# Bilinear sampling of a deformable convolution: hat weights on input rows replaced by ramps on differences of neighbouring rows

## The chip, the cores and the metric

The program runs on one core of a Trainium2 chip: TensorE (PE, matmul), VectorE (DVE), ScalarE (ACT), GpSimd (POOL), and SyncE (SP), which here only issues transfers. Times are device microseconds (us) of one launch. The time before is the median of three launches; the profile is of one further execution, whose span is its own.

## The reference

Four layers are applied to x of 16 images, 32 channels, 128 x 128, each as a residual on a group-normalised input. The change lies in layer 1, a deformable convolution with nine taps. Cut to what matters:

```python
y = weight * yk + y_new                 # row positions, one per image, tap, row and column
ys = jnp.clip(y_map, 0.0, Hi - 1.0)     # x positions are whole numbers: a column each
...
for dy in (0.0, 1.0):                   # the two rows next to y
    yi = y0 + dy
    w = 1.0 - jnp.abs(gy - yi)
    out = out + feat[:, yi, xc] * w
...
out = conv2d(deformed, dsc_w, dsc_b, stride=(K, 1))
return group_norm(out, gn_w, gn_b, gn_w.shape[0] // 4)
```

A sample at row position y of a column is a linear interpolation between two rows x[r]. It can be written in two ways over all 128 rows: as a sum of x[r] times the hat max(0, 1 - |y - r|), or as x[0] plus the sum of (x[r+1] - x[r]) times the ramp min(1, max(0, y - r)).

## The kernel before

The stages of the program run one after the other: layer 0, the offsets of layer 1, the scan of layer 1, the sampling of layer 1 (`layer1_sample`), layer 2, layer 3. The sampling goes image by image, 16 images of 32 blocks; a block is four output columns, that is 512 sample positions for each of the nine taps. The gather is a matmul: the stationary side is an input column `xt[:, :, xc]` (128 rows x 32 channels), the moving side the weights of all 128 rows for the 128 positions of a column.

For each block m the weights come from three places. For taps 0 to 3 (`near`, tile `ya`) PE spreads one row of the position map `Y` over 128 partitions with a one-hot matrix `sel` (L1121), ACT subtracts the row number and takes the absolute value on the way out of PSUM (L1122), and DVE makes the hat, min(d, 1) - 1 (`hats`, L1126). For taps 4 to 7 (tile `yd`) a transfer of 1 MB brings the positions already repeated over the partitions (`fetch`, L1111), ACT takes the absolute value (`absolutes`, L1242) and DVE makes the hat. Tap 8 (`eighth`, tile `h8`) is as `ya`, once for four blocks. The minus sign of the hat is in the convolution's weights `w4`, `w8`.

Then PE gathers (`taps`, L1133, 16 matmuls for taps 0 to 3 and 16 for taps 4 to 7), and DVE copies each result from PSUM to `ds` (L1280, L1286). For every four blocks there follow the last tap (L1307), the convolution over the taps (`convolve`, L1168, L1173, L1176), and transposes into the image's output `ob` (`turn`, L1185, L1186). While the next image runs, `finish` normalises `ob` piece by piece, one step after each block, adds the residual `xt` (L1233) and sends `ob` out by a transfer that POOL issues (L1234).

Order: the instructions of PE, DVE and ACT in the loop keep the program's order (`in_order`). SP's transfers are placed by the framework's scheduler; SP itself works through them in a fixed order, and a transfer that waits holds up those behind it. `yd` has four buffers, and the loads run three blocks ahead; `xt`, 2 MB per image in four quarters of 8 channels (L1099, rows of 512 bytes), has two buffers, as have `Y` and `Y8` (L1091, L1095). PSUM: two buffers `pb` for the spreads, two `pd` for gathers.

Two other lines are used below as measures: L797 in the scan loads a tile `dd` of 128 partitions from 8 rows of `dm`, each repeated 16 times, and L666 loads `xa` and `xb` in pieces of 72 and of 24 rows.

Of the kernel before, what the change touches and what calls it, by code (L numbers as in the profile page):

```python
# [10 lines left out]
F32 = mybir.dt.float32  # L11
AF = mybir.ActivationFunctionType
ALU = mybir.AluOpType
# [1017 lines left out]
def layer1_sample(tc, w, x1, x2, ymap, sb1, batches=range(B)):  # L1031
# [6 lines left out]


    nc = tc.nc  # L1040
    V, S, M = nc.vector, nc.scalar, nc.tensor.matmul
    W4 = 4 * HW
    NB = HW // 4
    batches = list(batches)
    with ExitStack() as ctx:
# [9 lines left out]
        nrow = load(nc, cp, w["nrow"], "nrow")  # L1055
        avg = cp.tile([P, P], F32, name="avg", tag="avg")
        V.memset(avg, 1.0 / P)

        sel = cp.tile([P, 32, P], F32, name="sel", tag="sel")

        cb = cp.tile([P, NG, 4, 2], F32, name="cb", tag="cb")
        with tc.tile_pool(name="ct", bufs=1) as tp:
            e32 = load(nc, tp, w["eye32"], "eye32")
            V.tensor_copy(sel, e32.unsqueeze(2).to_broadcast([P, 32, P]))
# [22 lines left out]
        def open_image(b):  # L1087
            im = images[b] = {}
            g, j = divmod(b, 4)
            im["Y"] = Y = yp.tile([P, W4], F32, name="Y", tag="Y")  # L1090
            nc.sync.dma_start(Y, ym(b)[0:4].rearrange("k (n f) -> (k n) f", f=W4))  # L1091
            im["Y8"] = Y8 = yp.tile([P, W4], F32, name="Y8", tag="Y8")
            y8 = ym(b)[8].rearrange("(s q f) -> q s f", q=4, f=W4)
            for q in range(4):
                nc.sync.dma_start(Y8[32 * q : 32 * q + 8], y8[q])  # L1095
            im["xt"] = xt = xp.tile([P, T, HW], F32, name="xt", tag="xt")
            xg = x1[g][T * j : T * j + T].rearrange("o (r c) -> r o c", c=HW)
            for q in range(4):
                nc.sync.dma_start(xt[:, 8 * q : 8 * q + 8], xg[:, 8 * q : 8 * q + 8])  # L1099

            s = cb[:, g, j, 0:1]
            im["w4"] = w4 = sp.tile([P, 2, T], F32, name="w4", tag="w4")
            V.tensor_scalar(w4, dw4[:, :, 0:T], s, -1.0, ALU.mult, ALU.mult)
            im["w8"] = w8 = sp.tile([P, P], F32, name="w8", tag="w8")
            V.tensor_scalar(w8, dw8, s, -1.0, ALU.mult, ALU.mult)

        def fetch(m):
            b, n = order[m]
# [3 lines left out]
                yd, ym(b)[4:8, n * W4 : n * W4 + W4].unsqueeze(0).to_broadcast([P, 4, W4])  # L1112
            )

        def spread(dst, Y, n, k):

            for h in range(2):
                pb = psb.tile([P, 2, W4], F32, name="pb", tag="pb")
                for a in range(2):
                    q = 32 * (2 * h + a)  # L1120
                    M(pb[:, a], sel[q : q + k, n], Y[q : q + k], start=True, stop=True)  # L1121
                S.activation(dst[:, 2 * h : 2 * h + 2], pb, AF.Abs, bias=nrow)  # L1122

        def hats(t):

            V.tensor_scalar(t, t, 1.0, 1.0, ALU.min, ALU.subtract)  # L1126

        def sample(pd, b, todo):

# [61 lines left out]
        def finish(b):  # L1191

            g, j = divmod(b, 4)
            im = images[b]
            ob, xt = im["ob"], im["xt"]
# [44 lines left out]
        def absolutes(m):  # L1240
            yd = blocks[m]["yd"]
            S.activation(yd, yd, AF.Abs, bias=nrow)  # L1242

        def near(m):
            b, n = order[m]
            blocks[m]["ya"] = ya = hp.tile([P, 4, W4], F32, name="ya", tag="ya")
            spread(ya, images[b]["Y"], n, 32)

        def eighth(b, s):
            h8 = hp.tile([P, 4, W4], F32, name="h8", tag="h8", bufs=2)  # L1250
            spread(h8, images[b]["Y8"], s, 8)
            images[b]["h8", s] = h8

        open_image(batches[0])
        NM = len(order)
        for m in range(min(3, NM)):
            fetch(m)
        with in_order(tc, nc.tensor, nc.vector, nc.scalar):
            eighth(batches[0], 0)
            near(0)  # L1260
            absolutes(0)
            near(1)
            hats(images[batches[0]]["h8", 0])
            hats(blocks[0]["ya"])
            hats(blocks[0]["yd"])
            done = iter(())
            for m in range(NM + 6):
                b, n = order[m] if m < NM else (None, m - NM)
                if m < NM:
                    bl = blocks[m]  # L1270
                    bl["ds"] = dp.tile([P, 2, W4], F32, name="ds", tag="ds", bufs=6)
                    if n == 12 and m + NB < NM:
                        open_image(order[m + NB][0])
                    if m + 3 < NM:
                        fetch(m + 3)
                    pd = taps(m, 0, bl["ya"])
                    if m + 1 < NM:
                        absolutes(m + 1)
                        hats(blocks[m + 1]["ya"])
                    V.tensor_copy(bl["ds"][:, 0], pd.rearrange("p i r -> p (i r)"))  # L1280
# [5 lines left out]
                    V.tensor_copy(bl["ds"][:, 1], pd.rearrange("p i r -> p (i r)"))  # L1286
                s, i = divmod(n, 4)
                if i == 0 and 4 <= m <= NM:
                    bb, nn = order[m - 4]
# [14 lines left out]
                elif i == 3 and m < NM:  # L1304
# [3 lines left out]
                    images[b]["ds8"] = ds8  # L1308
                    if m + 1 < NM:
                        nb_, nn = order[m + 1]  # L1310
                        hats(images[nb_]["h8", nn // 4])
                next(done, None)
            for _ in done:
                pass
# [982 lines left out]
def pack(inp):  # L2297
# [105 lines left out]
    w["nrow"] = -np.arange(P, dtype=f)[:, None]  # L2403

    def conv(a):
        return _diag(a.reshape(a.shape[0], a.shape[1], 9).transpose(1, 2, 0), 4)
# [97 lines left out]
```

## Time and profile before

| | us |
|---|---|
| three launches: median (lowest, highest) | 16867.01 (16856.64, 16888.87) |
| profiled execution, span | 16843.7 |
| layer 0, about 0 to 5600 | 5600 |
| offsets of layer 1, 5600 to 6050 | 450 |
| scan of layer 1, 6050 to 10,850 | 4800 |
| sampling of layer 1, 10,850 to 14,024 | 3174 |
| layer 2, 14,024 to 14,600 | 576 |
| layer 3, 14,600 to the end | 2243 |

The boundaries are read from the first and last instructions of the stages' lines and rounded. A row of instructions in the profile reads: line, engine, operation, output tile <- input tiles, output shape <- input shape, count; busy time in us and the mean of one in ns; idle time of the engine just before them, and who ended it. The stage is 512 blocks long. By the starts of L1242, one per block, an image takes 189 to 198 us, and four blocks some 23.4 us where nothing is late.

### The profile page before, as it was taken

What the parts mean: (1) busy time and instruction counts of PE and PEld (TensorE: products, weight loads), DVE (VectorE), ACT (ScalarE), POOL (GpSimd) and SP (SyncE); (2) the same over time, 40 slices, a digit from 0 to 9 for tenths busy, and PEclk for the clock granted to TensorE, in tenths of its full rate; (3) what the DMA queues carried; (4) which work ended last, traced back from release to release, by engine and by line L of the source; (5) the groups of instructions that cost most, each with busy time, mean ns of one, the idle gap of its engine ahead of it and who ended that gap; (6) DMA issues with size and microseconds to landing.
All of it is one profiled execution on the core that took longest, in us unless ns stands there. A gap on an engine that the chain in (4) does not pass through costs nothing. (4 is left out here: it accounts for less than half of the span.)

```text
span 16843.7 us, 301825 instructions
## 1 busy us (share of the span) xinstructions
PE 14662.1 (87%) x113386; PEld 5677.8 (34%) x113386; DVE 14631.9 (87%) x14520; ACT 12582.5 (75%) x25308; POOL 9561.6 (57%) x17517
## 2 busy tenths in 40 slices
PE   8999999989999888988888888899999997688966
PEld 3333333333333222222222222255555553234421
DVE  9999999999999669999999999888888887788622
ACT  8999999999999557777777677688898883466411
POOL 8999999999999238778887788500000000000012
PEclk9999999999999989899999999899999898788977
DMA  0000000000000854445454445578877789644456
GB/s 22 13 12 13 13 17 13 13 12 13 18 13 8 136 139 164 154 161 163 168 166 163 156 161 168 159 187 197 200 199 194 193 192 195 129 79 83 79 147 201
DMA packets 1553471, 1898.99 MB, mean 113 GB/s; under 512 B 158053, under 2 KB 879710, under 8 KB 1543239
## 3 DMA queue, kind: packets, MB, share of 16 engines
q1 hardware_dynamic: 1440582, 1701.94, 38.7%
q0 software_dynamic: 31552, 127.40, 2.1%
q10 hardware_dynamic: 79872, 50.36, 1.2%
q8 instruction: 892, 14.61, 0.4%
q14 instruction: 573, 4.69, 0.1%
HBM read 1560.92 MB, written 229.64 MB: 106 GB/s over the span
## 5 line engine op out<-in xcount | busy, mean ns | idle before, releaser
L235 POOL TENSOR_SCALAR Rp<-su,nv 128x128 f32<-128x128 f32 x15360 | 5406.1, 371 | 167.7 <-PE pS L241 132.9
L239 ACT ACTIVATE Ra<-su,bv 128x128 f32<-128x128 f32 x15360 | 4625.8, 389 | 405.9 <-PE pS L241 402.6
L224 DVE TENSOR_TENSOR Rd<-pu,nv 128x2048 f32<-128x2048 f32 x2176 | 4856.6, 2275 | 19.6 <-PE pS L241 18.6
L241 PE MATMUL pS<-Rd,zw 128*32 128x512 f32 x17408 | 2794.8, 606 | 380.1 <-DVE Rd L224 379.4
L828 DVE TENSOR_TENSOR_SCAN hh<-dd,state,pd 128x512 f32<-128x512 f32 x2304 | 2823.3, 1267 | 152.6 <-PE py L862 9.6
L849 POOL TENSOR_TENSOR hh<-hh,bc 128x2048 f32<-128x2048 f32 x512 | 2319.0, 4530 | 451.2 <-DVE state L836 437.9
L1234 POOL DMA_DIRECT2D x<-ob x64 | 92.4, 1443 | 3106.4 <-DVE ob L1233 2769.9
L813 PE MATMUL pd<-du,spread 32*128 32x512 f32 x4608 | 1348.8, 659 | 553.3 <-DVE hh L828 545.7
L805 ACT ACTIVATE dd<-dd,m_a 128x512 f32<-128x512 f32 x2304 | 1513.1, 713 | 328.5 <-DMA dd<-dm 322.4
L823 DVE TENSOR_TENSOR pd<-pd,bc 128x1024 f32<-128x1024 f32 x1152 | 1401.0, 1216 | 53.4 <-ACT bc L786 51.4
L241 PE MATMUL pS<-Rp,zw 128*32 128x512 f32 x7680 | 1310.7, 597 | 25.3 <-POOL Rp L235 25.2
L1242 ACT ACTIVATE yd<-yd,nrow 128x2048 f32<-128x2048 f32 x512 | 1239.7, 2421 | 47.6 <-DMA yd<-ymap 47.5
L1122 ACT ACTIVATE ya<-pb,nrow 128x1024 f32<-128x1024 f32 x1024 | 1188.4, 1251 | 86.5 <-PE pb L1121 85.4
L241 PE MATMUL pS<-Ra,zw 128*32 128x512 f32 x7680 | 1235.7, 600 | 0.0
L1121 PE MATMUL pb<-Y,sel 32*128 32x512 f32 (+1 forms) x5120 | 1083.6, 742 | 167.5 <-ACT ya L1122 164.2
L241 PEld LDWEIGHTS pS<-Rd,zw 128*32 128x32 f32 x17408 | 580.8, 109 | 1487.5 <-DVE Rd L224 928.7
L813 PEld LDWEIGHTS pd<-du,spread 32*128 32x128 f32 x4608 | 372.8, 190 | 1594.7 <-DVE hh L828 714.4
L1126 DVE TENSOR_SCALAR yd<-yd 128x2048 f32<-128x2048 f32 x512 | 724.2, 1414 | 191.8 <-ACT yd L1242 190.9
L1126 DVE TENSOR_SCALAR ya<-ya 128x2048 f32<-128x2048 f32 x512 | 756.7, 1478 | 9.2 <-ACT ya L1122 7.6
L1133 PE MATMUL pd<-ya,xt 128*32 128x128 f32 x16384 | 690.7, 311 | 42.7 <-DVE ds L1286 31.3
L1133 PEld LDWEIGHTS pd<-yd,xt 128*32 128x32 f32 x16384 | 539.2, 178 | 469.9 <-issue 231.5
L1839 PE MATMUL ps<-t,W 128*128 128x512 f32 x1280 | 627.8, 637 | 64.2 <-DVE W L1819 56.5
(426 smaller groups left out, 23147.3 us busy)
## 6 DMA issues: line engine op xcount, KB each, us to landing
dd<-dm SPq DMA_DIRECT2D x2304, 256.0 KB
yd<-ymap SPq DMA_DIRECT2D x512, 1024.0 KB
hw<-x SPq DMA_DIRECT2D x192, 512.0 KB
dm<-dt POOLq DMA_DIRECT2D x192, 256.0 KB, 3.6
w<-d SPq DMA_DIRECT2D x512, 73.1 KB
xb<-tok SPq DMA_DIRECT2D x248, 144.0 KB
x<-in_x SPq DMA_DIRECT2D x64, 512.0 KB
x<-o SPq DMA_DIRECT2D x128, 256.0 KB
```

Source lines behind the costliest of these rows:

```text
L224: nc.vector.tensor_tensor(R, st["pu"].unsqueeze(1).to_broadcast([P, 4, 4, HW]), nv[:, :, i::32].rearrange("p t q -> p q t").unsqueeze(3).t ...
L235: nc.gpsimd.tensor_scalar(R[:, q, k], su[:, k], 3.4028234e38, nv[:, k, c], ALU.min, ALU.max)
L239: nc.scalar.activation(R[:, q, k], su[:, k], AF.Relu, bias=bv[:, k, c])
L241: nc.tensor.matmul(st["pS"][32 * q : 32 * q + 32], zw[:, 31 - i : 63 - i], R[:, q], start=first, stop=False, tile_position=(0, 32 * q), sk ...
L805: S.activation(dd[:, r], dd[:, r], AF.Exp, scale=acol[:, dr, d : d + 1])
L813: nc.tensor.matmul(pd[:, a], spread[e, k], st["du"][n][e], start=True, stop=True)
L823: V.tensor_mul(pd, pd, bm.unsqueeze(1).to_broadcast([P, 2, CH]))
L828: V.tensor_tensor_scan(hh[:, r, s], dd[:, r, s], pd[:, a, s], st["state"][:, 4 * i + r : 4 * i + r + 1], ALU.mult, ALU.add,)
L849: G.tensor_mul(hh, hh, st["bc"][1, n].unsqueeze(1).to_broadcast([P, 4, CH]))
L1126: V.tensor_scalar(t, t, 1.0, 1.0, ALU.min, ALU.subtract)
L1133: M(pd[32 * q : 32 * q + 32, i], xt[:, :, xc], h, start=True, stop=True, tile_position=(0, 32 * q),)
L1242: S.activation(yd, yd, AF.Abs, bias=nrow)
```

## The change

- `hats` on rows becomes ramps on differences. The weights are now min(1, max(0, y - r)) for r = 0 to 126, and row 127 carries a constant weight of one for row 0 of the image. `xt` therefore holds rows 1 to 127 in partitions 0 to 126 and row 0 in partition 127 (two transfers per quarter, 127 rows and one row); POOL then subtracts the unshifted rows, which come in a tile `xq` of their own with two buffers (`quarter`, `differ`). The next image's subtractions are written in blocks 24 to 27 of the image before it; POOL's instructions keep the program's order too.
- The residual in `finish` reads a fresh load of `xq`, since `xt` no longer holds the input.
- The row number is subtracted by the spread product: `Y` is split in `Y0` and `Y1`, with 16 rows and a row of ones in each group of 32 partitions, and `sel` has the step (0, -1, -2, ..., and 1 for row 127) in the row that meets the ones. The spread has 17 rows in place of 32 (or of 8 for tap 8). `Y8` has its 8 rows twice.
- `ya` is made by one DVE operation from PSUM (two for a block, 128 x 1024 each) in place of an ACT and a DVE pass.
- For `yd` and `h8` ACT takes Relu in place of Abs and DVE takes the minimum with one.
- The two copies of gathers to `ds` move from DVE to ACT, and `ramps` stands behind the next spread in the program.

```diff
-            im["Y"] = Y = yp.tile([P, W4], F32, name="Y", tag="Y")
-            nc.sync.dma_start(Y, ym(b)[0:4].rearrange("k (n f) -> (k n) f", f=W4))
...
+            for h, key in enumerate(("Y0", "Y1", "Y8")):
+                im[key] = Y = yp.tile([P, W4], F32, name=key, tag=key)
+                for q in range(4):
+                    p = 32 * q
+                    if h < 2:
+                        nc.sync.dma_start(Y[p : p + 16], yk[q, h])
+                    else:
+                        nc.sync.dma_start(Y[p : p + 8], y8[q])
+                        nc.sync.dma_start(Y[p + 8 : p + 16], y8[q])
+                nc.sync.dma_start(Y[16:P:32], w["one_rows"])
...
-                nc.sync.dma_start(xt[:, 8 * q : 8 * q + 8], xg[:, 8 * q : 8 * q + 8])
+                o = slice(8 * q, 8 * q + 8)
+                nc.sync.dma_start(xt[0 : P - 1, o], xg[1:P, o])
+                nc.sync.dma_start(xt[P - 1 : P, o], xg[0:1, o])
...
+        def quarter(b, q):
+            g, j = divmod(b, 4)
+            xq = xp.tile([P, 8, HW], F32, name="xq", tag="xq")
+            xg = x1[g][T * j + 8 * q : T * j + 8 * q + 8].rearrange("o (r c) -> r o c", c=HW)
+            nc.sync.dma_start(xq, xg)
+            return xq
+
+        def differ(b, q):
+            xt = images[b]["xt"][0 : P - 1, 8 * q : 8 * q + 8]
+            G.tensor_sub(xt, xt, quarter(b, q)[0 : P - 1])
...
-                    M(pb[:, a], sel[q : q + k, n], Y[q : q + k], start=True, stop=True)
-                S.activation(dst[:, 2 * h : 2 * h + 2], pb, AF.Abs, bias=nrow)
-
-        def hats(t):
-
-            V.tensor_scalar(t, t, 1.0, 1.0, ALU.min, ALU.subtract)
+                    M(pb[:, a], sel[q : q + 17, n], Y[q : q + 17], start=True, stop=True)
+                if whole:
+                    V.tensor_scalar(dst[:, 2 * h : 2 * h + 2], pb, 0.0, 1.0, ALU.max, ALU.min)
+                else:
+                    S.activation(dst[:, 2 * h : 2 * h + 2], pb, AF.Relu)
+
+        def clamps(t):
+
+            V.tensor_scalar_min(t, t, 1.0)
...
+                xq = quarter(b, q)
...
-                V.tensor_add(ob[:, o], ob[:, o], xt[:, o])
+                V.tensor_add(ob[:, o], ob[:, o], xq)
...
-            S.activation(yd, yd, AF.Abs, bias=nrow)
+            S.activation(yd, yd, AF.Relu, bias=step)
...
-        with in_order(tc, nc.tensor, nc.vector, nc.scalar):
+        with in_order(tc, nc.tensor, nc.vector, nc.scalar, nc.gpsimd):
...
+                    if 24 <= n < 28 and m + NB < NM:
+                        differ(order[m + NB][0], n - 24)
...
-                    if m + 1 < NM:
-                        absolutes(m + 1)
-                        hats(blocks[m + 1]["ya"])
-                    V.tensor_copy(bl["ds"][:, 0], pd.rearrange("p i r -> p (i r)"))
+                    S.copy(bl["ds"][:, 0], pd.rearrange("p i r -> p (i r)"))
                     if m + 2 < NM:
                         near(m + 2)
+                    if m + 1 < NM:
+                        ramps(m + 1)
                     pd = taps(m, 4, bl["yd"])
                     if m + 1 < NM:
-                        hats(blocks[m + 1]["yd"])
-                    V.tensor_copy(bl["ds"][:, 1], pd.rearrange("p i r -> p (i r)"))
+                        clamps(blocks[m + 1]["yd"])
+                    S.copy(bl["ds"][:, 1], pd.rearrange("p i r -> p (i r)"))
```

More of the change, by code (lines that the diff above doesn't have):

```diff
@@ L1040, in layer1_sample @@
     nc = tc.nc
-    V, S, M = nc.vector, nc.scalar, nc.tensor.matmul
+    V, G, S, M = nc.vector, nc.gpsimd, nc.scalar, nc.tensor.matmul
     W4 = 4 * HW
@@ L1054, in layer1_sample @@
         ident = load(nc, cp, w["ident"], "ident")
-        nrow = load(nc, cp, w["nrow"], "nrow")
+        step = load(nc, cp, w["step"], "step")
         avg = cp.tile([P, P], F32, name="avg", tag="avg")
         V.memset(avg, 1.0 / P)
-        sel = cp.tile([P, 32, P], F32, name="sel", tag="sel")
+        sel = cp.tile([P, 16, P], F32, name="sel", tag="sel")
         cb = cp.tile([P, NG, 4, 2], F32, name="cb", tag="cb")
         with tc.tile_pool(name="ct", bufs=1) as tp:
-            e32 = load(nc, tp, w["eye32"], "eye32")
-            V.tensor_copy(sel, e32.unsqueeze(2).to_broadcast([P, 32, P]))
+            pick = load(nc, tp, w["pick"], "pick")
+            srow = load(nc, tp, w["step_row"], "step_row")
+            V.tensor_add(
+                sel, pick.unsqueeze(2).to_broadcast([P, 16, P]),
+                srow.unsqueeze(1).to_broadcast([P, 16, P]),
+            )
             selq = load(nc, tp, w["selq"], "selq")
@@ L1089, in open_image @@
             g, j = divmod(b, 4)
-            im["Y"] = Y = yp.tile([P, W4], F32, name="Y", tag="Y")
-            nc.sync.dma_start(Y, ym(b)[0:4].rearrange("k (n f) -> (k n) f", f=W4))
-            im["Y8"] = Y8 = yp.tile([P, W4], F32, name="Y8", tag="Y8")
+            yk = ym(b)[0:4].rearrange("k (h n f) -> k h n f", h=2, f=W4)
             y8 = ym(b)[8].rearrange("(s q f) -> q s f", q=4, f=W4)
-            for q in range(4):
-                nc.sync.dma_start(Y8[32 * q : 32 * q + 8], y8[q])
+            for h, key in enumerate(("Y0", "Y1", "Y8")):
[8 more added lines that the diff above has]
+                nc.sync.dma_start(Y[16:P:32], w["one_rows"])
             im["xt"] = xt = xp.tile([P, T, HW], F32, name="xt", tag="xt")
@@ L1098, in open_image @@
             for q in range(4):
-                nc.sync.dma_start(xt[:, 8 * q : 8 * q + 8], xg[:, 8 * q : 8 * q + 8])
+                o = slice(8 * q, 8 * q + 8)
+                nc.sync.dma_start(xt[0 : P - 1, o], xg[1:P, o])
+                nc.sync.dma_start(xt[P - 1 : P, o], xg[0:1, o])
             s = cb[:, g, j, 0:1]
             im["w4"] = w4 = sp.tile([P, 2, T], F32, name="w4", tag="w4")
-            V.tensor_scalar(w4, dw4[:, :, 0:T], s, -1.0, ALU.mult, ALU.mult)
+            V.tensor_scalar_mul(w4, dw4[:, :, 0:T], s)
             im["w8"] = w8 = sp.tile([P, P], F32, name="w8", tag="w8")
-            V.tensor_scalar(w8, dw8, s, -1.0, ALU.mult, ALU.mult)
+            V.tensor_scalar_mul(w8, dw8, s)
+        def quarter(b, q):
[7 more added lines that the diff above has]
+            G.tensor_sub(xt, xt, quarter(b, q)[0 : P - 1])
         def fetch(m):
@@ L1113, in fetch, with spread @@
             )
-        def spread(dst, Y, n, k):
+        def spread(dst, Y, n, whole):
             for h in range(2):
@@ L1194, in finish @@
             im = images[b]
-            ob, xt = im["ob"], im["xt"]
+            ob = im["ob"]
             st = sp.tile([P, 8, 6], F32, name="st", tag="st")
@@ L1238, in finish, with ramps @@
                 yield
-        def absolutes(m):
+        def ramps(m):
             yd = blocks[m]["yd"]
-            S.activation(yd, yd, AF.Abs, bias=nrow)
+            S.activation(yd, yd, AF.Relu, bias=step)
         def near(m):
@@ L1246, in near @@
             blocks[m]["ya"] = ya = hp.tile([P, 4, W4], F32, name="ya", tag="ya")
-            spread(ya, images[b]["Y"], n, 32)
+            spread(ya, images[b][f"Y{n // 16}"], n % 16, True)
         def eighth(b, s):
             h8 = hp.tile([P, 4, W4], F32, name="h8", tag="h8", bufs=2)
-            spread(h8, images[b]["Y8"], s, 8)
+            spread(h8, images[b]["Y8"], s, False)
             images[b]["h8", s] = h8
         open_image(batches[0])
+        for q in range(4):
+            differ(batches[0], q)
         NM = len(order)
@@ L1257, in layer1_sample @@
             fetch(m)
-        with in_order(tc, nc.tensor, nc.vector, nc.scalar):
+        with in_order(tc, nc.tensor, nc.vector, nc.scalar, nc.gpsimd):
             eighth(batches[0], 0)
             near(0)
-            absolutes(0)
+            ramps(0)
             near(1)
-            hats(images[batches[0]]["h8", 0])
-            hats(blocks[0]["ya"])
-            hats(blocks[0]["yd"])
+            clamps(images[batches[0]]["h8", 0])
+            clamps(blocks[0]["yd"])
             done = iter(())
@@ L1310, in layer1_sample @@
                         nb_, nn = order[m + 1]
-                        hats(images[nb_]["h8", nn // 4])
+                        clamps(images[nb_]["h8", nn // 4])
                 next(done, None)
@@ L2402, in pack @@
     w["dsc_rows"] = np.tile(np.stack([i["gn_w"], i["gn_b"]])[None], (P, 1, 1))
-    w["nrow"] = -np.arange(P, dtype=f)[:, None]
+    w["step"] = -np.arange(P, dtype=f)[:, None]
+    w["step"][P - 1] = 1.0
+    w["pick"] = np.tile(np.eye(T, dtype=f)[:, :16], (4, 1))
+    w["step_row"] = np.zeros((P, P), f)
+    w["step_row"][16::T] = w["step"][:, 0]
+    w["one_rows"] = np.ones((4, 4 * HW), f)
     def conv(a):
```

## The prediction

> **What bounds the kernel now.** I read the stages first (busy time of each engine in the window of the sampling stage), then the groups of that stage, then its waits, then its transfers. The change touches only the stage from 10,850 to 14,024 us of the profiled execution.
>
> ```profile
> 10850.00:14024.00 3174.00, 2894.07 (x44856) 1697.65 (x44856) 2740.74 (x2926) 2798.29 (x2065) 91.49 (x63) 0.90 0.78 193
> ```
> ```profile
> L1242 ACT ACTIVATE yd<-yd,nrow 128x2048 f32<-128x2048 f32 x326 | 789.6, 2422 | 29.3 <-DMA yd<-ymap 29.2
> L1122 ACT ACTIVATE ya<-pb,nrow 128x1024 f32<-128x1024 f32 x654 | 760.2, 1250 | 52.9 <-PE pb L1121 51.9 <-ACT yd L1242 0.7
> L1126 DVE TENSOR_SCALAR ya<-ya 128x2048 f32<-128x2048 f32 x327 | 481.1, 1471 | 3.9 <-ACT ya L1122 3.1
> L1126 DVE TENSOR_SCALAR yd<-yd 128x2048 f32<-128x2048 f32 x327 | 465.5, 1424 | 117.4 <-ACT yd L1242 116.9
> L1286 DVE COPY ds<-pd 128x512 f32<-128x512 f32 x327 | 246.4, 753 | 33.9 <-PE pd L1133 33.7
> L1280 DVE COPY ds<-pd 128x512 f32<-128x512 f32 x326 | 240.3, 737 | 64.6 <-PE pd L1133 64.2
> L1307 ACT COPY ds<-pd 128x512 f32<-128x512 f32 x81 | 72.1, 890 | 18.8 <-PE pd L1133 18.4
> ```
>
> The first fence gives the stage's length, then busy us of PE, weight loads, DVE, ACT, POOL, then granted clock, DMA share and GB/s: three engines are busy 86 to 91% together and POOL is nearly free. The groups are of the inner window 11,600 to 13,600 us (326 blocks, 6.13 us each). There ACT was busy 895.9 us in the first 1000, or 5.5 us of a block; it makes both distances (2.42 + 2 x 1.25) while DVE waits for it (116.9 us). So ACT is the tightest of three nearly equal engines. DMA stops the stage rarely: ACT waited for a yd tile 8 times in 2000 us, 29.2 us in all (its column of idle time), each 5.1 us at most; in the one I followed in the timeline SP had just issued the xt loads.
>
> **The transfers**, in two windows: 9100 to 9300 us (the scan before the stage) and 405 to 412 us (a load of x in 512-byte rows).
>
> ```profile
> DMA packets 15930, 31.21 MB, mean 156 GB/s; under 512 B 1320, under 2 KB 1320, under 8 KB 15919
> ...
> dd<-dm SPq DMA_DIRECT2D x96, 256.0 KB
> dm<-dt POOLq DMA_DIRECT2D x9, 256.0 KB, 3.8
> xb<-tok SPq DMA_DIRECT2D x10, 144.0 KB
> xa<-tok SPq DMA_DIRECT2D x5, 144.0 KB
> kept<-t SPq DMA_DIRECT2D x5, 144.0 KB
> xb<-tok SPq DMA_DIRECT2D x9, 48.0 KB
> xa<-tok SPq DMA_DIRECT2D x5, 48.0 KB
> ```
> ```profile
> DMA packets 2974, 1.52 MB, mean 217 GB/s; under 512 B 37, under 2 KB 2973, under 8 KB 2973
> ...
> q1 hardware_dynamic: 2973, 1.50, 75.9%
> ```
>
> No transfer listed in the first has rows under 512 B, so its 1320 short packets are the marks with which each DMA engine reports its share done: they count engines. dm (128 rows) at 16, dd (8 rows, each repeated 16 times) at 8, and the 144 KB and 48 KB ones (72 and 24 rows) at 12 give 9x16 + 96x8 + 34x12 = 1320, exactly. 72 rows use 12 engines though 16 exist, so a transfer is cut into equal shares: the largest number up to 16 that divides its rows. The second gives the price of a 512-byte packet: 0.759 x 16 engines x 7 us / 2973 = 28.6 ns of one engine.
>
> **The change, part by part.**
>
> *Engines, per block.* ACT loses the two ya activations (2 x 1.25) and gains two copies (0.89, L1307's form): -0.7 us. DVE loses the ya pass (1.47) and both copies (0.74 + 0.75) and gains two 128x1024 passes out of PSUM. No row has that operation; above, L823, a 128x1024 DVE operation on PSUM, took 1216 ns, and below, half of L224's 128x2048 from PSUM is 1138 ns; I take 1.2: +2.4, net -0.56. The Abs becomes Relu at the same shape, and the subtraction of the row number moves into the spread product, a 17th row in the same 32-row tile: nothing on PE, whose matmuls go by their 512 columns (K = 8 and K = 32 share the L1121 row). PE keeps some 4.7 us of a block (in one stretch of the timeline without waits: 8 x 1.1 + 4 x 1.07 for taps and spreads of four blocks, 5.7 for the rest, 18.8 in four). So a block ends between 4.7 and 6.13 us, with ACT and DVE near 4.8; as before, chains between three equal engines will eat half of the room: 5.6. That is 512 x 0.53 = 270 us gained (bounds 0 and 730).
>
> *POOL.* 64 subtractions of 127x1024. L847, the same size, took 2345 ns: 150 us on an engine that has 91 of 3174 us to do. Hidden, except four at the start (the first taps wait). If they stop DVE, up to 150; I take 0, since DVE has 0.8 us of slack a block.
>
> *SP queue.* Per image there are 8 xq loads, 4 xt loads of 127 rows and 4 of one row, 27 small Y loads. xq has two buffers, so the loads for images' differences 1 to 3 and the first of the next finish stand in SP in a row, each waiting for a POOL subtraction or a DVE add before it. From the last add: DMA issue on POOL 1.4, subtraction 2.35, then three rounds of load (3.8 us, the dm row) and subtraction; some 14 us until the next yd load is issued, which is needed 2 blocks (11 us) later and takes 4 to 6 to land. Stall 9 us per image against some 4 now (the xt loads): +80 us for 16.
>
> *The xt load.* Before: 128 rows, 16 engines, 1024 packets x 28.6 / 16 = 1.8 us a quarter. Now 127 rows, and 127 is prime. Bounds: 16 engines (1.8 us) or one (1016 x 28.6 ns = 29.1 us). The nearest rows, 72 and 24 on 12 engines and 8 on 8, follow the divisor, so I take one engine: 116 us for the four quarters of an image, in the ring that also carries 1/16 of every yd load. A yd tile is complete only when that share is, so each yd issued after a quarter lands after it.
>
> The Trainium skill, "DMA: Bandwidth & Descriptors", section "Why a DMA increments its semaphore by 16 and not by 1", states the same rule and names 127 partitions as one engine. No row here shows 127; by that page the sum is the forecast, without it rival B.
>
> What this stops: at the start of an image SP issues, in the order the scheduler gave the changed program, quarter 0, 1, yd(3), quarter 2, yd(4), quarter 3, yd(5). yd(5) lands after 4 x 29.1 plus three shares of 32 packets x 109 ns (22 us around 12,200: 0.738 x 16 x 22 / 2391), 127 us; ACT wants it in block 4, at 4 x 5.6 + 1.7 = 24 us. So 103 us lost per image, as only three yd tiles are ahead. It happens 14 times (images 2 to 15). At the start nothing is ahead: xt was issued at 10,847.8 and the first taps ran at 10,858.6; with 116 us of loads and a subtraction, +108. Image 1's quarters follow at once: 95. In all 14 x 103 + 203 = 1645 us.
>
> *Sum.* 16,843.7 (the profiled execution, 23 below the median of three) + 1645 + 80 - 270 = 18,299; at the median 18,320 us.
>
> **The rivals.**
>
> A (forecast, 0.86): one engine, loads in ring order: 18,320. Own range: 26 to 35 ns a packet (-170 to +420), engine gain 0 to 450: 17,950 to 18,900. Granted clock after each stop (0.62 in the 10 us after the idle of 12,200) adds little, some 3 us a stop.
>
> B (0.08), faster: 127 rows run on all 16 engines after all. Then the xt load costs as before and what is left is -270 + 80 + 15 at the start: 16,690 (16,450 to 16,900). For it: only 8, 24, 72 and 128 were seen. It decides if a quarter lands within some 8 us.
>
> C (0.05): one engine, but it takes turns between transfers, so yd slips through. Then its own load binds: 116 + 32 x 32 packets x 109 ns (112) + xq 15 = 243 us an image, against 195 now; 16 x 243 + 108 - 3174 = +820: 17,690; with yd packets at 81 ns (402 GB/s in the best slice of that window) some 17,240. Against it: yd already waited behind the xt loads (29.2 us).
>
> D (0.01): the SP chain alone, with B's loads but 20 us longer per image: 17,010.
>
> **How the numbers follow.** Prediction A, 18,320. The range takes A's and C's, 17,400 to 18,900, some 0.85 of the chance. What the measurement can tell from no change is about 0.2%, 34 us. Faster needs B: 0.07. Same 0.02. Slower 0.91.
>
> **What would show it.** Right: the busy share of ACT, DVE and PE in the stage falls below 0.7; ACT's wait at the Relu of yd for "DMA yd" grows from 47.5 to over 1000 us, in three long waits at each image's first blocks; the 4-quarter xt group takes over 100 us; away from them blocks take about 5.6 us. L1280/L1286 copies stand under ACT at 0.6 to 0.9, and ya under DVE from PSUM at 1.2 us. Wrong: first taps before 10,900 us, no yd wait over 10 us, and a stage under 3174 us (B); or even blocks of 7.5 us all through the image (C).

## The result, and the profile after

| | before | changed |
|---|---|---|
| median of four launches, us | 16865.85 | 18515.39 |
| lowest, highest | 16856.64, 16888.87 | 18468.52, 18582.8 |
| profiled execution, span | 16843.7 | 18533.0 |

The ratio is 1.098 (95% interval 1.0953 to 1.1008): slower by about 1650 us. Nearly all of it lies in the sampling stage. From the first ACT pass over `yd` to the last one it takes 4772.3 us, before 3123.9, which is 1648 us more; the first of these passes starts 44 us later, and what follows the stage is the same to 3 us.

The groups of the changed kernel that answer to those shown of before, from the page's costliest groups (busy us, mean ns | idle us before it and who ended it). L1269 is the Relu of `yd` on ACT (before: L1242), L1152 its clamp on DVE, L1146 the new DVE pass out of PSUM:

```profile
L1269 ACT ACTIVATE yd<-yd,step 128x2048 f32<-128x2048 f32 x512 | 1248.4, 2438 | 1538.7 <-DMA yd<-ymap 1538.6
L1146 DVE TENSOR_SCALAR ya<-pb 128x1024 f32<-128x1024 f32 x1024 | 1298.4, 1313 | 735.7 <-PE pb L1144 734.7
L1152 DVE TENSOR_SCALAR yd<-yd 128x2048 f32<-128x2048 f32 x512 | 701.2, 1370 | 1429.0 <-ACT yd L1269 1428.7
```

ACT stands 1539 us before a `yd` transfer that has not landed, and DVE stands behind ACT for nearly as long: one stall, seen on two engines. Where it begins is seen in SP's timeline around the start of an image (start, duration until SP went on, line, output<-input, count; L1110 is the 127-row quarter of `xt`, L1111 its one-row partner, L1134 a `yd` load):

```profile
12206.81 0.25 SPq L1110 DMA_DIRECT2D xt<-x  x1
12207.11 27.01 SPq L1111 DMA_DIRECT2D xt<-x  x1
12234.17 0.41 SPq L1110 DMA_DIRECT2D xt<-x  x1
12234.70 25.65 SPq L1134 DMA_DIRECT2D yd<-ymap  x1
12260.40 0.80 SPq L1111 DMA_DIRECT2D xt<-x  x1
12261.25 0.43 SPq L1110 DMA_DIRECT2D xt<-x  x1
12261.72 29.85 SPq L1111 DMA_DIRECT2D xt<-x  x1
12291.67 0.39 SPq L1134 DMA_DIRECT2D yd<-ymap  x1
12292.10 0.35 SPq L1110 DMA_DIRECT2D xt<-x  x1
12292.50 30.19 SPq L1111 DMA_DIRECT2D xt<-x  x1
```

The four quarters take 12,206.81 to 12,322.69, or 116 us. Each issue of L1110 is short, but whatever SP issues next is held for 26 to 30 us, so the stream of `yd` loads, one per block, stops four times. What the transfers did meanwhile, 12,220 to 12,300 us (the GB/s of 40 slices of 2 us, then the sum):

```profile
GB/s 20 20 28 20 20 20 20 22 20 20 20 20 20 20 20 20 20 20 20 20 100 164 100 195 18 29 20 20 20 20 20 20 20 20 20 20 124 166 158 107
DMA packets 3816, 3.53 MB, mean 44 GB/s; under 512 B 59, under 2 KB 2790, under 8 KB 3814
```

A steady 20 GB/s between short bursts, in rows of 512 bytes: some 25.6 ns a packet. It was 193 GB/s over this stage before.

For the rest of the bill, the blocks of an image are summed by their place in it (distances between the starts of the ACT pass over `yd`, mean of images 2 to 15, us; the last three columns are experiments told below):

| blocks | before | changed | e1 | e3 | e6 |
|---|---|---|---|---|---|
| 0 to 2 | 17.1 | 17.4 | 17.3 | 16.8 | 18.8 |
| 3 to 5 | 19.1 | 111.8 | 20.9 | 18.8 | 21.9 |
| 6 to 25 | 120.9 | 130.6 | 130.7 | 120.9 | 124.3 |
| 26 | 7.7 | 10.6 | 10.8 | 103.3 | 3.9 |
| 27 to 31 | 31.5 | 28.6 | 28.6 | 31.5 | 26.3 |
| whole image | 196.3 | 299.1 | 208.3 | 291.4 | 195.2 |
| first image | 189.1 | 389.2 | 208.7 | 272.5 | 187.8 |
| first to last start | 3123.9 | 4772.3 | 3321.0 | 4538.5 | 3098.6 |

Before, the images took 189 to 201 us each (not 189 to 198). Blocks 3 to 5 hold 92.7 of the 102.8 us that an image grew by. The first image, with nothing loaded ahead, grew by 200. The next largest part is blocks 6 to 25: they are far from the loads, and still 9.7 us slower, where they were foreseen to be faster. The windows of the stage and of a stretch behind the stall (length, busy us of PE, weight loads, DVE, ACT, POOL; granted clock, DMA share, GB/s) show that no engine fills the stage:

```profile
10850.00:15700.00 4850.00, 3189.86 (x44928) 1925.46 (x44920) 2580.60 (x2423) 2240.53 (x2067) 258.67 (x130) 0.72 0.55 141
12330.00:12480.00 150.00, 132.49 (x1851) 79.34 (x1855) 114.12 (x108) 97.80 (x90) 15.36 (x8) 0.77 0.78 205
```

Over the stage PE is busy 66%, DVE 53%, ACT 46%. In the stretch without a stall DVE and ACT have room (76% and 65%) and PE is busy 88%, but at a granted clock of 0.77, against 0.90 before. What happens there is seen in the timeline of PE and DVE (start, duration, engine, line; in brackets the idle time before it):

```profile
12387.60 1.21 PE L1144 MATMUL pb<-Y,sel 17*128 17x512 f32 x8
...
12388.68 0.68 DVE L1212 COPY ob<-pt 128x512 f32<-128x512 f32 x1
12388.90 1.21 PE L1159 MATMUL pd<-yd,xt 128*32 128x128 f32 x32
12389.28 1.28 DVE L1260 TENSOR_TENSOR ob<-ob,xq 128x1024 f32<-128x1024 f32 x1
12390.48 2.33 DVE L1146 TENSOR_SCALAR ya<-pb 128x1024 f32<-128x1024 f32 x2
...
12391.74 2.33 PE L1144 MATMUL pb<-Y,sel 17*128 17x512 f32 x8 [1.64 <-DVE ya L1146]
...
12394.01 2.01 PE L1159 MATMUL pd<-ya,xt 128*32 128x128 f32 x32
...
```

This is the block in which tap 8 is spread as well. PE needs the two PSUM buffers `pb` for it, which now DVE empties, and DVE has first copied the output tile and done a step of the finish. PE waits 1.64 us, and from then on the same work takes nearly twice as long (the 16 gathers of four taps, counted x32 in the row, 2.01 instead of 1.21 us). The clock record of the trace shows this in blocks 6 to 25 of images 2 to 16: full clock for some 17 us, then mostly 6.8 or 10.2 us at half, once in four blocks. The kernel before has such a wait in the same block, for ACT, and half clock behind it; but its wait lasts 1.1 us in the median, and its halves 3.4 or 6.8 us.

### The profile page after: what moved, and what is told of

It is laid out like the page before. It is cut to its first block, busy times and chain, and to the rows that moved or that the text cites. A ratio compares the mean times of both kernels' runs of the same rounds, so it can differ in the third digit from the quotient of the medians.

```text
span 18533.0 us, 302854 instructions
## 1 busy us (share of the span) xinstructions
PE 14983.1 (81%) x113386; PEld 5909.8 (32%) x113386; DVE 14472.6 (78%) x14008; ACT 12025.5 (65%) x25308; POOL 9713.7 (52%) x17581
## 4 chain that ended last, share of the span: by engine, by line
DVE 33%; PE 29%; SPq 12%; ACT 9%; issue 8%; DMA 5%; POOL 3%; DVEq 0%; ACTq 0%; POOLq 0%
DVE hh L828 11%; DVE Rd L224 7%; SPq L1111 7%; PE pS L241 6%; ACT Ra L239 5%; DVE pd L823 5%; PE pd L1159 4%; PE ps L1868 4%; PE pb L1144 3%; POOL Rp L235 3%; SPq L1134 2%; DVE ya L1146 2%; DMA yd<-ymap 1%; PE pd L813 1%; PE ps L544 1%
## 5 line engine op out<-in xcount | busy, mean ns | idle before, releaser
L1269 ACT ACTIVATE yd<-yd,step 128x2048 f32<-128x2048 f32 x512 | 1248.4, 2438 | 1538.7 <-DMA yd<-ymap 1538.6
L1146 DVE TENSOR_SCALAR ya<-pb 128x1024 f32<-128x1024 f32 x1024 | 1298.4, 1313 | 735.7 <-PE pb L1144 734.7
L1152 DVE TENSOR_SCALAR yd<-yd 128x2048 f32<-128x2048 f32 x512 | 701.2, 1370 | 1429.0 <-ACT yd L1269 1428.7
L1159 PE MATMUL pd<-ya,xt 128*32 128x128 f32 x16384 | 746.8, 331 | 738.9 <-ACT ds L1315 621.4
L1159 PE MATMUL pd<-yd,xt 128*32 128x128 f32 x16384 | 768.2, 337 | 663.4 <-DVE yd L1152 649.9
L1144 PE MATMUL pb<-Y,sel 17*128 17x512 f32 x5120 | 1115.9, 795 | 172.1 <-DVE ya L1146 116.3
L1159 PEld LDWEIGHTS pd<-yd,xt 128*32 128x32 f32 x16384 | 614.9, 181 | 1168.2 <-ACT ds L1307 603.5
L1159 PEld LDWEIGHTS pd<-ya,xt 128*32 128x32 f32 x16384 | 613.2, 179 | 990.2 <-ACT ds L1315 630.4
```

What stands on the lines that cost most here:

```text
L1144: M(pb[:, a], sel[q : q + 17, n], Y[q : q + 17], start=True, stop=True)
L1146: V.tensor_scalar(dst[:, 2 * h : 2 * h + 2], pb, 0.0, 1.0, ALU.max, ALU.min)
L1159: M(pd[32 * q : 32 * q + 32, i], xt[:, :, xc], h, start=True, stop=True, tile_position=(0, 32 * q),)
```

## The experiments

The times of before beside these runs were 16,888.04, 16,853.15, 16,870.69 and 16,906.07 us (medians of 13, 23, 11 and 23 launches, for e1 to e4, e5 and e6, e7 and e8, e9 and e10). A ratio is to the kernel before of the same group, so runs of different groups are best compared by their ratios.

**e1_112_15: the same load in two pieces whose row counts have large divisors.**

```diff
-                nc.sync.dma_start(xt[0 : P - 1, o], xg[1:P, o])
+                nc.sync.dma_start(xt[0:112, o], xg[1:113, o])
+                nc.sync.dma_start(xt[112 : P - 1, o], xg[113:P, o])
```

> The changed kernel with each 127-row load cut into 112 rows (16 engines) and 15 rows (15 engines). One-engine theory: the three long waits for yd in blocks 3 to 5 of an image (52, 31 and 31 us between block starts, some 95 us too much) go, 14 times, and some 190 us at the start; an image takes 200 to 205 us, the total 16,900 to 17,000. Rival (the 4 MB of extra xq loads an image, or the SP chain, hold up yd): the waits stay and the total is over 18,000. Second question: if the engines had gained what I forecast, it would be some 16,690; the blocks outside the waits in the changed kernel say they did not.

Measured: 17,097.15 us (four launches), ratio 1.0132 (1.0111 to 1.0153).

**e2_122_5: pieces of 122 and 5 rows** (the same edit with 122 and 123 in place of 112 and 113).

> The changed kernel with each 127-row load cut into 122 rows (2 x 61, so two engines) and 5 rows. Divisor theory: a quarter takes half as long, 13 us; yd tiles 3, 4 and 5 of an image land some 30, 46 and 62 us after its start, so about 33 us are lost per image in place of 95, and 90 at the start: total 17,400 to 17,600. Rival 1 (any count that is not a multiple of 16 costs the same): 18,500. Rival 2 (only a single engine is slow, or the shares are uneven rather than few): 16,950.

Measured: 17,663.56 us, one launch, some 60 us above the expected range. The group of the Relu in the stage, e1 first, then e2:

```profile
L1270 ACT ACTIVATE yd<-yd,step 128x2048 f32<-128x2048 f32 x512 | 1273.3, 2487 | 95.0 <-DMA yd<-ymap 94.2 <-DVE yd L1153 0.5
```
```profile
L1270 ACT ACTIVATE yd<-yd,step 128x2048 f32<-128x2048 f32 x512 | 1245.4, 2432 | 792.5 <-DMA yd<-ymap 792.2
```

ACT's wait is 1539 us with 127 rows, 792 with 122 + 5, and 94 with 112 + 15; against e1 the total is 1418, 566 and 0 us longer. The bytes and rows are the same in all three, and e2 has as many transfers as e1; what differs is into how many equal shares a piece can be cut (1; 2 and 5; 16 and 15). So the stall is the divisor of 127. But e1 stayed some 100 us above what was expected of it: with the stall gone, an image still takes 208.3 us, with 130.7 of them in blocks 6 to 25, as in the changed kernel.

**e3_before_127: the kernel before, with nothing but its `xt` load split into 127 rows and one row.**

```diff
-                nc.sync.dma_start(xt[:, 8 * q : 8 * q + 8], xg[:, 8 * q : 8 * q + 8])
+                o = slice(8 * q, 8 * q + 8)
+                nc.sync.dma_start(xt[0 : P - 1, o], xg[0 : P - 1, o])
+                nc.sync.dma_start(xt[P - 1 : P, o], xg[P - 1 : P, o])
```

> The kernel before with nothing changed but the xt load: rows 0 to 126 and row 127 as two transfers. One-engine theory: four quarters need over 100 us of one engine, some 95 us lost per image and 100 at the start: total 18,200 to 18,600. Rival (the loss needs the other new transfers, or the early place of the xt load): within 100 us of 16,866.

Measured: 18,414.85 us, one launch, inside the expected range. The Abs of `yd` in the stage of e3:

```profile
L1244 ACT ACTIVATE yd<-yd,nrow 128x2048 f32<-128x2048 f32 x512 | 1232.9, 2408 | 1572.5 <-DMA yd<-ymap 1572.5
```

This split alone costs 1527 us. The table shows the stall moved to block 26, where this kernel's loads stand in SP's queue: 103.3 us there in place of 7.7, and the other rows of an image as before. Ramps, differences and the moved copies are not needed for it.

**e4_tap8_own_psum: e1, with tap 8 spread through the PSUM tiles `po` and `pt` instead of `pb`,** in two halves in the third and fourth block of each four, and its clamp one block later.

```diff
-            spread(h8, images[b]["Y8"], s, False)
+            for q in (2 * half, 2 * half + 1):
+                p8 = pso.tile([P, 4, HW], F32, name="p8", tag=("po", "pt")[q % 2])
+                M(
+                    p8.rearrange("p i r -> p (i r)"), sel[32 * q : 32 * q + 17, s],
+                    Y[32 * q : 32 * q + 17], start=True, stop=True,
+                )
+                S.activation(h8[:, q], p8.rearrange("p i r -> p (i r)"), AF.Relu)
```

> As e1, and tap 8's spread goes through the two PSUM banks of the convolution and the transposes, in two halves in blocks 2 and 3, in place of the two buffers that it shares with ya. Theory (TensorE waits at tap 8 for DVE to free the shared buffers, and each such wait sets the granted clock to one half for 7 to 10 of some 24 us): the clock of the stage goes from about 0.8 to 0.9, four blocks take 22 us, the total is 16,500 to 16,750. Rival (the clock is low because a product of 17 rows counts for less than one of 32, or DVE is the bound): the clock stays near 0.8 and the total within 60 us of e1.

Measured: 16,953.35 us (ten launches), ratio 1.0032 (1.0015 to 1.0049), 144 us under e1. The windows of 11,000 to 14,000 us, before first, then e1, then e4:

```profile
11000.00:14000.00 3000.00, 2759.06 (x42870) 1619.03 (x42866) 2609.80 (x2785) 2667.53 (x1969) 88.83 (x60) 0.91 0.78 194
```
```profile
11000.00:14000.00 3000.00, 2768.33 (x40620) 1680.66 (x40618) 2346.01 (x2169) 2056.45 (x1869) 220.54 (x112) 0.83 0.80 204
```
```profile
11000.00:14000.00 3000.00, 2803.18 (x42900) 1647.26 (x42900) 2526.17 (x2276) 2195.03 (x2216) 244.16 (x119) 0.90 0.85 216
```

From e1 to e4 the clock goes from 0.83 to 0.90, and in the same 3000 us PE does 5.6% more matmuls (42,900 against 40,620) in nearly the same busy time. PE's waits for `pb` in these windows, in the same order (waiting engine and line <- who ended the wait: us in all, times, longest):

```profile
PE pb L1121 <- ACT ya L1122: 152.7, 118, 5.9
```
```profile
PE pb L1145 <- DVE ya L1147: 114.8, 101, 1.8
```
```profile
PE pb L1145 <- DVE ya L1147: 12.3, 23, 1.9
```

With the waits for DVE nearly gone, blocks 6 to 25 fall from 130.7 to 122.5 us. So tap 8's place in the shared buffers is what made most of these blocks' loss. But the first line shows that such waits are not new: before, PE waited there for ACT, as often, at a clock of 0.91. What is new is their length. In blocks 6 to 25 (images 2 to 16) the waits over 0.8 us last 1.07 us in the median before and 1.60 us in e1, and the half clock of these blocks adds up to 20 us an image before, 47 in e1 and 23 in e4. The run removes the waits and the low clock together and does not price them apart. It ended above the 16,500 to 16,750 that had been expected: the clock came back, the time foreseen with it did not.

The Trainium skill, "TensorE: Matmul & The Clock Gate", section "A second HAM failure mode: psum-queue depth-cycling", tells of a kernel in which short idle gaps between groups of matmuls, from cycling through PSUM buffers, make the clock swing between half and full. This case agrees: 0.83 in e1 with gaps of some 1.6 us once in four blocks, 0.90 in e4 nearly without them. The length of the gap seems to matter: with gaps of 1.1 us in the same place the kernel before kept 0.91.

**e5_early_xt and e6_yd5: what was left in SP's queue.** e5 is e4 with the next image's loads and differences moved; e6 is e5 with a fifth `yd` buffer, loads one block earlier, and `ds` cut from six to five buffers to make room.

```diff
-                    if n == 12 and m + NB < NM:
+                    if n == 2 and m + NB < NM:
                         open_image(order[m + NB][0])
-                    if 24 <= n < 28 and m + NB < NM:
-                        differ(order[m + NB][0], n - 24)
+                    if n in (4, 6, 8, 10) and m + NB < NM:
+                        differ(order[m + NB][0], n // 2 - 2)
```

> Tap 8 in its own banks as in e4_tap8_own_psum, and the next image's xt loads and differences moved from blocks 12 and 24 to 27 up to blocks 2 and 4, 6, 8, 10, one per two blocks, ahead of the stretch in which the finish of the image before uses the two xq buffers. Theory: the long blocks left in that run (block 26 and the first blocks of an image) are SP standing in front of xq loads whose buffers are still held, so that the yd loads behind are late. Then ACT's wait for yd falls from 93 us in 2000 to under 40, an image from about 200 to 190, and the total from 16,953 to 16,750 to 16,880. Rival: the 8 differences land on blocks that are long anyway through the rstd chain (9 to 11), or the loads merely move; then within 30 us of 16,953.

> As e5_early_xt, with five yd buffers instead of four and each yd load issued four blocks ahead instead of three (ds has five buffers instead of six). Theory: one more block of lead (5 us) covers what SP is held up by, so that ACT's wait for yd is nearly gone: under 15 us in 2000, and 30 to 80 us less than e5_early_xt. Rival: ACT and DVE bind by then, and the time is within 20 us of e5_early_xt.

Measured: e5 16,894.8 us, ratio 1.0019 (1.0011 to 1.0028); e6 16,848.27 us, ratio 0.9998 (0.9985 to 1.0011); twelve launches each. The expectation for e5 failed: ACT's wait for `yd` in the stage fell only from 132 to 96 us, an image took 201.7 us in the profiled execution, where 190 was expected and e4 had 197.9, and the total came out just above the range. Part of that stall had only moved, to block 7, which became 9 to 16 us. e6 took it away and is 47 us under e5, as expected of it. Its Relu group from the page, and its stage:

```profile
L1270 ACT ACTIVATE yd<-yd,step 128x2048 f32<-128x2048 f32 x512 | 1281.7, 2503 | 21.1 <-DMA yd<-ymap 21.0
```
```profile
10892.00:13991.00 3099.00, 2899.15 (x44698) 1709.92 (x44694) 2624.08 (x2374) 2296.27 (x2312) 243.42 (x124) 0.91 0.84 219
```

With 21 us of waits for `yd` left and the clock at 0.91, the changed kernel takes the time of the kernel before: 195.2 us an image against 196.3. It does have a faster rhythm, 21.4 us for the last four blocks of an image against 24.1 before (means of images 2 to 15), but it is slower in the first blocks and in blocks 8 to 12 (7 to 9 us), where the previous image's finish runs.

**e7, e9 and e10: moving the finish and the clamp away from DVE.** All start from e6. e7 does tap 8's clamp and the finish's last addition on POOL, with the loads one block earlier and the differences in blocks 5, 6, 9 and 10; e9 does the finish's scale and bias on ACT, eight activations of 128x128 for each quarter; e10 is e9 with no finish step in every fourth block.

```diff
-                    clamps(images[b]["h8", s])
+                    G.tensor_scalar_min(images[b]["h8", s], images[b]["h8", s], 1.0)
...
-                V.tensor_add(ob[:, o], ob[:, o], xq)
+                G.tensor_add(ob[:, o], ob[:, o], xq)
```
```diff
-                V.tensor_mul(ob[:, o], ob[:, o], col[0])
-                yield
-                V.tensor_add(ob[:, o], ob[:, o], col[1])
-                yield
+                for c in range(8 * q, 8 * q + 8):
+                    S.activation(
+                        ob[:, c], ob[:, c], AF.Identity,
+                        bias=bi[:, c // 4, c % 4 : c % 4 + 1], scale=sc[:, c // 4, c % 4 : c % 4 + 1],
+                    )
+                    if c % 4 == 3:
+                        yield
```
```diff
-                next(done, None)
+                if i != 1 or n < 2:
+                    next(done, None)
```

> e6_yd5 with two kinds of work moved from DVE to POOL, which is busy 150 us of 2000 there: the clamp of tap 8's weights (128x2048, 1.6 us on DVE, 8 an image) and the last addition of the finish (128x1024, 1.5 us, 4 an image); the xt loads one block earlier, the differences in blocks 5, 6, 9, 10. Theory: in the first half of an image, where the finish runs, blocks last 7 to 10 us instead of 5 because DVE has the finish on top of its 4.1 us a block, so what is taken from DVE comes off the time: up to 19 us of an image's 193, of which half is expected, 16 x 9 = 150 us: 16,848 to 16,650 to 16,760. Rival: PE (busy 94%) binds, or POOL's slower passes (2.9 us for 128x1024, up to 4.5 for 128x2048) and its queue hold the ob buffers and DVE's memory accesses: within 40 us of 16,848, or above it.

> e6_yd5 with the finish's scaling and bias (two DVE passes of 128x1024, 1.5 us each, 4 times an image) done by eight ACT activations of 128x128 a quarter instead. Theory: DVE sets the blocks in which the finish runs, and POOL could not take its work (e7_pool_clamp_add) because POOL's passes slowed DVE's; ACT has room (busy 74%) and does not. 12 us of DVE an image go, some 12 (32 x 0.39 us) come to ACT; half of it is expected in the time: 16,848 to 16,700 to 16,800. Rival: ACT's activations are in order before the yd and ds work, and the chain ACT, DVE, PE gets no shorter: within 40 us of 16,848.

> e9_finish_on_act with the finish's steps left out of every fourth block (where DVE also moves the output tile out of PSUM), so that its 23 steps fill some 30 of 32 blocks. Theory as there: work spread evenly over blocks waits less; 20 to 60 us under e9_finish_on_act. Rival: blocks that were free of it and ran at 5.0 us become longer by what the others gain: within 20 us of it.

Measured: e7 16,955.31 us, ratio 1.0049 (1.003 to 1.0068); e9 16,937.57 us, ratio 1.0016 (1.0003 to 1.003); e10 16,915.96 us, ratio 1.0009 (0.9996 to 1.0022). None is faster than before, where e6 had 0.9998. The theories of e7 and e9 fell. The rival of e9, within 40 us of e6, holds by the ratios (some 30 us slower) and not by the medians (89 us), which come from different groups. e10 decides nothing: it is 22 us under e9, at the edge of what its theory and its rival allow, and the two intervals overlap. Why e7 got worse is in its timeline:

```profile
12995.02 6.04 POOL L1327 TENSOR_SCALAR h<-h 128x2048 f32<-128x2048 f32 x1 [15.62 <-ACT h L1287]
12995.07 2.64 DVE L1147 TENSOR_SCALAR ya<-pb 128x1024 f32<-128x1024 f32 x2 [0.40 <-PE pb L1145]
12997.75 4.40 DVE L1153 TENSOR_SCALAR yd<-yd 128x2048 f32<-128x2048 f32 x1
...
13002.66 2.80 DVE L1147 TENSOR_SCALAR ya<-pb 128x1024 f32<-128x1024 f32 x2
13005.38 1.20 DVE L1153 TENSOR_SCALAR yd<-yd 128x2048 f32<-128x2048 f32 x1
```

While POOL clamps for 6.04 us, DVE's clamp of `yd` takes 4.40 us; with POOL idle the same instruction takes 1.20 here. It ends 1.1 us after POOL does, and so do the others: of the 82 clamps of `yd` in this trace that begin during a clamp of POOL and outlast it, nearly all end 1.1 us after it. DVE's clamp thus stands until POOL's pass is over. The 285 clamps of `yd` with nothing on POOL beside them take 1.22 us in the median, the 226 with some 2.88. The DVE pass that reads PSUM is not slowed (2.64 and 2.80 for two). Over the kernel the mean of DVE's clamp rose from 1360 to 1970 ns, or 312 us for 512, more than the 1.6 us x 128 + 1.5 us x 64 = 301 us that were taken off DVE. The Trainium skill, "GPSIMD Engine Reference", section "1. Specifications", says that POOL shares its SBUF interfaces with VectorE and that some forms of DVE instructions contend for them; the durations above agree with it.

What binds e6 and e9 in the first half of an image is not settled. PE is busy for 94% of e6's stage, at a clock of 0.91, and is the likeliest; no run took work from PE.

**e8_xt_on_pool: the changed kernel, with the 127-row load issued from POOL's queue.**

```diff
-                nc.sync.dma_start(xt[0 : P - 1, o], xg[1:P, o])
+                nc.gpsimd.dma_start(xt[0 : P - 1, o], xg[1:P, o])
```

> The changed kernel with only the 127-row xt load issued from POOL's queue instead of SP's; it still runs on one DMA engine. Theory: the stall of 95 us an image comes from what stands behind those loads in SP's queue: SP was held 27 to 30 us at each of them, and the yd loads were issued only then. From another queue the yd loads are issued on time and share the one engine packet by packet; then ACT's wait for yd falls from 1539 us to under 500, and the total from 18,515 to 17,300 to 17,700. Rival: the engine serves what it was given in order over all queues, so that every yd load's sixteenth share stands behind the quarters whoever issues them: ACT's wait stays over 1300 us and the total within 150 us of 18,515.

Measured: 18,033.4 us, one launch. ACT's wait for `yd` (us in all, times, longest):

```profile
ACT yd L1269 <- DMA yd<-ymap: 945.4, 162, 35.0
```

Between the two expectations: the wait is 945 us, where the theory wanted under 500 and the rival over 1300. An image falls from 299.1 to 259.2 us, but the first one grows from 389.2 to 467.9: PE waits 278.7 us there for POOL's subtractions, which stand behind POOL's own issues. The waits are no longer three long ones: they are spread over the image, 35.0 us at most. A quarter takes 36 us from issue to landing at the start, where nothing else moves, and 49 us in the stage (medians); alone it moves at 18 GB/s (10,905 to 10,917 us, 5.8% of the time of 16 engines, or about one). So SP's held queue was a part of the stall, some 40 of 103 us an image. That the larger part comes from the share which every `yd` load has on the one engine that the quarter occupies is likely but not shown, since more than the queue changed: these packets have 4 KB and not 512 bytes, and POOL works 6.7 us at each issue, beside which 64 of DVE's clamps of `yd` take 4.2 us in the mean instead of 1.3.

## Why the prediction was right, and where it was not

The forecast was 18,320 us, and 18,515 was measured, in rival A's own range of 17,950 to 18,900. Its three terms against the profiled execution, from the table above (14 images, the first and the last one):

| term | predicted | measured | from |
|---|---|---|---|
| stall of the `xt` loads | 14 x 103 + 203 = 1645 | 14 x 92.7 + 200 = 1498 | blocks 3 to 5, first image |
| chain of `xq` loads in SP's queue | 80 | 14 x 2.9 = 41 | block 26 |
| engine gain | -270 | 14 x (0.3 + 9.7 - 2.9) + 9 = 108 | the other blocks, last image |
| start of the stage | 0 | 44 | first pass over `yd` |
| sum | 1455 | 1691 | spans differ by 1689.3 |

The last term is not the change's: the scan, whose code is the same, ended 48 us later in this execution, and in the twelve profiled executions it ends anywhere from 10,812 to 10,935 us. That the total came within 195 us is in part luck: stall and chain were taken 186 us too large together, which hid half of the 378 us by which the engine term missed.

- **One engine for 127 rows: right.** It was read from 1320 short packets of transfers with other row counts, and e1, e2 and e3 show that the divisors of the row count decide. SP issued quarters and `yd` loads in just the order that had been foreseen, and the four quarters took 116 us, the number worked out.
- **The price per packet: some 25.6 ns, not 28.6.** The packets of one engine overlap: their durations add up to 32 ns a packet at 20 GB/s (12,222 to 12,258 us), so a price read from the busy share is too high. The 116 us still came out by luck: four loads at 25.6 ns are 104 us, and the shares of `yd` and the issues between the quarters fill the rest. The stall itself was 92.7 us, not 103.
- **How the load stops the stream: partly right.** The prediction let SP go on issuing and the `yd` shares queue up on the ring. SP's next issue was held too, 26 to 30 us each time. In e8 an image is 40 of 103 us shorter without the held queue; what makes the rest is not shown.
- **Rival C was wrong for one queue.** For two, its 243 us an image, for an engine that takes turns, stands beside 259.2 in e8; no run shows that its sum is what makes that time.
- **Rival B did not come about, and its time was wrong too.** e1 is nearly its case (loads on 15 and 16 engines, no long stall), but gives 17,097 and not 16,690, because B rested on the term that failed.
- **The term that failed is the engine gain.** "So a block ends between 4.7 and 6.13 us, with ACT and DVE near 4.8", taken at 5.6, was to save 270 us; blocks away from the stall got longer, 6.46 us in the mean of the 29 against 6.11, and the term is +108. The DVE pass out of PSUM took 1.31 us, not 1.2 (116 us more of DVE in 1024 passes). One step that the sum left out is PE's wait for `pb` at tap 8: DVE now empties `pb`, with its output copy and finish in front, the wait grew from 1.1 to 1.6 us, and the half clock behind it doubled. e4 gives back 8.2 of the 9.7 us of blocks 6 to 25. That reaches the time of before, and not the gain: 20 blocks at 5.6 us would be 112 us, and e4 has 122.5. For this rest the likeliest account is PE. The prediction's own first row has PE busy 2894 us in 512 blocks, 5.65 us each, at a clock of 0.90: PE was the busiest engine, not ACT, and a block of 5.6 us left it no idle time. The floor of 4.7 us came from one stretch without waits. In e6 PE is still busy 5.7 us of a block's 6.1, but no run took work from PE, so this is not shown. The bounds of the gain, 0 and 730, excluded a loss without naming what excludes it. The remark on the clock after each stop, "adds little, some 3 us a stop", looked at the long stops; the short waits of every fourth block were the costly ones.
- **The chain of `xq` loads: right in kind, half the size.** Block 26 is 2.9 us longer; it is 3.9 us in e6, where the loads stand earlier.
- **POOL's subtractions: hidden, as taken.** They take 2.96 us, not 2.35. What they do to DVE, taken as 0 of up to 150 us, is small: 30 of the 512 clamps of `yd` run beside one and take 1.99 us in the mean, the others 1.33, or an estimated 20 us in all.

## What to carry to other kernels

Cutting one row off a 128-row load is a change of the transfer, not of the arithmetic: look at the row count's divisors before anything else, since 112 + 15 rows cost 2 us an image in the blocks where 127 cost 93. When a PSUM buffer passes from one engine to another, list what stands before the new reader on its engine: here PE's wait grew by half a microsecond, and the half clock behind it doubled. And before pricing an even trade between engines, here two passes from ACT to DVE and two copies back, divide the third engine's busy time by the blocks: PE's 5.65 us a block was above the forecast 5.6, and the trade was worth nothing even in e6.

## What the runs showed of the hardware that had not been expected

- SP goes on issuing only 26 to 30 us after a one-engine load of 1016 packets, even if the next transfer is a 4 KB row.
- The 127-row load moves at 20 GB/s in rows of 512 bytes (some 25.6 ns a packet), and at 18 GB/s in the packets of 4 KB that it has when issued from POOL (e8).
- PE's waits of 1.6 us in every fourth block go with 6.8 or 10.2 us of half clock each (e1, blocks 6 to 25: 56 of 58 waits); waits of 1.1 us with 3.4 or 6.8 us, or with none (before: 42 and 17 of 59). The clock of the stage is 0.83 and 0.91.
- A DVE clamp of 128x2048 f32 that begins during a POOL pass ends about 1.1 us after that pass: 4.40 us in place of 1.20 in e7. A DVE pass out of PSUM beside the same POOL pass kept its 1.3 us.
